# Two attentions per image on one core: own blocks mirrored from one half, and the last chunks of the second attention alternating with the next image's first chunks

## The chip, the cores and the metric

The kernel runs on one core of a Trainium2 chip. A core has a matrix engine (TensorE, PE in the profile; PEld is its loading of weights), VectorE (DVE), ScalarE (ACT), GpSimd (POOL) and SyncE (SP), which here only issues transfers. Transfers between the on-chip memory and DRAM (DMAs) are issued by an engine's instruction queue, here SP's almost always, and run on 16 DMA engines of the core. The metric is the device time of one execution, in microseconds (us). The median of three runs before the change is 1761.54 us (1758.81 to 1763.01).

## The reference

```python
B, C, S = 8, 128, 48;  N = S * S                     # 2304 positions
# layer 0: group norm, 32 rows of position table appended, q, k, v = leaky_relu(W x + b)
attn = einsum('bkn,bkm->bnm', q, k) / sqrt(128)      # masked to m <= n
out1 = einsum('bnm,bvm->bvn', softmax(attn) * mask, v);  x = x + out1
# layer 1, on tokens t of 128 channels
xh = layer_norm(t)
t = t + softmax(xh @ xh.T) @ xh                      # no mask: the matrix of logits is symmetric
wx = batch_norm(layer_norm(t) @ W.T)
y[i] = sigmoid(wx[i] + y[i-1] @ V.T)                 # recurrence over the 2304 tokens
t = t + y
```

Everything is fp32. Per image there are two attentions over 2304 positions, the first causal, the second full with a symmetric matrix of logits.

## The kernel before, in words

The 2304 positions are 18 blocks of 128, taken in six chunks (`NQ`) of three blocks (`QB`), 384 columns (`QC`). An attention's chunk j is a list of items. For each item TensorE makes the logits of one block of rows against the chunk's columns (tile `s`), ScalarE exponentiates them into one of six tiles `p`, and TensorE multiplies `p` with the values into the chunk's result `o` (one of two buffers). `Causal` does this for the first attention (L1018, L1020, L1029): its own three blocks are 384, 256 and 128 columns wide, GpSimd applies the triangle, and VectorE adds up the `p` for the sums of the softmax (L1040, L1044). `Full` does the second (L1217, L1219, L1231). There a block above the diagonal is computed once: VectorE transposes its exponentials in 32x32 pieces into a tile `t` (L1188), SP stores three such blocks to DRAM (`e`, L1168) and loads them back later in the order that completes the transpose (`g`, three buffers, L1159), and they serve as items "turned" of the later chunk, which need no logits (L1227). The three own blocks of a chunk, those on and beside the diagonal, are all computed directly at 384 columns: both halves.

The order of all instructions is written by the program itself. The items of all batches stand in one list, `stream`: causal chunks of a batch, then its full chunks, with the first three items of the next batch's first causal chunk set among the last six of the full part. The logits of an item are issued three items (`LAG`) ahead of its product. All other work (group norm, projection to q, k, v, normalization, transposed stores and loads, results) is in chains of steps; `Stream` keeps a model of the time and of when each engine is free, and runs a step when the model's time has come to it, or at once when an item needs it (`st.finish`). Each engine executes its own list in this order. A step that issues a DMA puts it at its place in the issuing engine's queue, where it waits for what it needs with all that stands behind it.

`project` makes q, k and v of a chunk (L879, L882, then an addition at L884 into a tile z and the leaky ReLU at L889), the first three of the next batch from full chunk 4 on. `Causal.after` takes a chunk's result: VectorE turns it (L958), SP stores and reloads it (`o_d`, `to_c`, L966 and L972) except for the last chunk, the residual and the layer norm follow (L1091, L920, L934), and TensorE transposes it into `xh` (L939, L1110). `xhT` and `xh` have one buffer, so the next batch's may be written only when the full part of this batch is done. `Full.after` copies the result (L1248), divides, adds the residual, and SP stores the turned tokens and reloads them (`t_d`, `rs`, then `t2x`, `scale`; L1291 to L1300) for the product with W (`wx`, L1306). After the eighth batch comes the recurrence.

Of the kernel before, what the change touches and what calls it, by code (L numbers as in the profile page):

```python
# [604 lines left out]
def fast_path(ctx: ExitStack, tc: tile.TileContext, x, pe, w_ffn, out, x_tok, w_qkv, w_pos, v_t, gamma_beta, flag):  # L605
# [61 lines left out]
    with ExitStack() as actx:  # L667
# [187 lines left out]
        def project(b, n):  # L855
# [18 lines left out]
            def part(j):  # L874
                def f():
# [7 lines left out]
                    z = chunk_tile("z", f"z_{b}_{n}_{j}")  # L883
                    nc.vector.tensor_add(z, ps[:, :QC], c["pb"][:, j, :])  # L884
# [3 lines left out]

                    nc.vector.scalar_tensor_tensor(dst, z, 0.01, z, ALU.mult, ALU.max)  # L889
# [97 lines left out]
        t1_tok, x_hat, normed_chunks = {}, {}, {}  # L987

        class Causal:
# [57 lines left out]
            def after(self, j, o):  # L1047
# [52 lines left out]
                def normed():  # L1100
                    if j == 0:
                        x_hat[b] = (
                            big.tile([P, NB, P], F32, tag="xhT", name=f"xhT_{b}"), big.tile([P, N], F32, tag="xh", name=f"xh_{b}")
                        )
# [7 lines left out]
                def shifted():  # L1112
# [4 lines left out]
                c["chain"] = normed_chunks[b, j] = st.add([  # L1117
# [6 lines left out]
                    (normed, 0.0, [("DVE", 1.1)]),  # L1124
                    (back, 0.35, [("ACT", 0.5)]),
                    (shifted, 0.0, [("POOL", 1.2)]),
                ], max(at, st.free["DVE"]) + 0.2 - st.now)

        class Full:
# [13 lines left out]
            def items():  # L1143
                chunks = []
                for j in range(NQ):
                    behind = list(range(j + 1, NQ))
                    ahead = [("direct", QB * n + g) for n in ([0] + behind if j == 0 else behind + [j]) for g in range(QB)]
# [3 lines left out]
                    chunks.append([w for _, w in sorted(both, key=lambda e: e[0])])  # L1151
                return listed(chunks)

            def load(self):
# [3 lines left out]
                for r in range(R):  # L1158
                    nc.sync.dma_start(  # L1159
                        g[ts(r, SQ)].rearrange("c a j m r -> c a (j m r)"),  # L1160
                        d.rearrange("(a c) b f -> b c a f", a=R)[r],
                    )
                self.loaded[i, j] = g

            def store(self):
                j, n, t, at = self.to_store.popleft()
                d = dpool.tile([P, R, QB * QB * SQ], F32, tag=f"e_{j}_{n}", name=f"e_{self.b}_{j}_{n}")
                nc.sync.dma_start(d, t.rearrange("p b j m r -> p b (j m r)"))  # L1168
                self.stored[j, n] = d, max(at, st.now)

            def prefetch(self):
# [3 lines left out]
                if n < len(self.pairs) and n < self.used + 3 and self.pairs[n] in self.stored:  # L1175
                    if self.stored[self.pairs[n]][1] + 6.0 <= st.now:
                        self.load()

# [17 lines left out]
            def begin(self, j, what, first):  # L1196
# [3 lines left out]
                if first and b + 1 < B:  # L1200
                    if j == 1:
                        norm_chain[b + 1] = st.add(group_norm(b + 1))
                    if j == NQ - 2:
# [3 lines left out]
                if what[0] == "turned":  # L1207
# [5 lines left out]
                    return self.loaded[i, j][:, :, g, :, :].rearrange("p a m r -> p m a r"), 0.0  # L1213
                m = what[1]
                xh = x_hat[b][1]
                s = psum_s(f"s1_{b}_{j}_{m}")
                nc.tensor.matmul(s[:, :QC], xh[:, ts(m, P)], xh[:, ts(j, QC)], start=True, stop=True)  # L1217
                p = pp.tile([P, QC], F32, tag="p", name=f"p1_{b}_{j}_{m}")
                nc.scalar.activation(p, s[:, :QC], AF.Exp, bias=shift)  # L1219
# [397 lines left out]
```

## Time and profile before

| what | us |
|---|---|
| median of the runs | 1761.54 |
| profiled execution, its own time | 1763.07 |
| its span, first to last instruction | 1761.4 |
| TensorE busy | 1733.7 (98%) |
| VectorE busy | 1159.5 (66%) |
| ScalarE busy | 718.9 (41%) |
| GpSimd busy | 321.0 (18%) |
| s of the second attention (L1217), 1008 passes | 409.3 |
| its o, direct (L1231), 1008 passes | 402.4 |
| its o, turned (L1227), 720 passes | 281.4 |
| VectorE's transposes for the turned blocks (L1188), 360 | 186.1 |

An fp32 matmul is two passes, and both are counted. Busy time of an engine is the union of its instructions; the end of a matmul is modelled, so that neighbours overlap in it, and the distance between starts tells more. The chain that ended last names at each step what released the work, so its shares say where time taken away is time gained. A wait that the profile puts down to an engine costs only where that engine is on the chain. The granted TensorE clock was 0.991 of full speed.

### The profile page before, as it was taken

To read this page: it belongs to the slowest core of one execution; us is meant where nothing else is said; L and a number is where in the kernel's file an instruction comes from. 1 tells how busy PE (TensorE), PEld (TensorE's weight loads), DVE (VectorE), ACT (ScalarE), POOL (GpSimd) and SP (SyncE) were. 2 spreads that over 40 slices of the span, in tenths; PEclk is the share of its full clock that TensorE was granted. 3 is DMA by queue.
4 is the path that set the end of the run, shared out by engine and by line. 5 is a ranking of instruction groups with operands and counts; after the bars stand their busy time and mean duration, and the time that the engine had idled before them with its cause. 6 is when DMAs were issued, how large, how long until landed. Compare 5 with 4: busy or idle time off the path is not lost.

```text
span 1761.4 us, 21442 instructions
## 1 busy us (share of the span) xinstructions
PE 1733.7 (98%) x6134; PEld 1082.0 (61%) x6135; DVE 1159.5 (66%) x3163; ACT 718.9 (41%) x1332; POOL 321.0 (18%) x397
## 2 busy tenths in 40 slices
PE   8999999999999999999999999999999999999986
PEld 5666666656666566666666566665666666665565
DVE  4875569655886459755696557864587556974357
ACT  2344334443344424443244433444344432444345
POOL 1131002300132001410024001320014100240006
PEclk7999999999999999999999999999999999999998
DMA  3415673157533684156731575335941568216768
GB/s 128 144 32 185 174 202 117 63 178 208 161 93 110 182 223 138 41 178 178 205 117 61 181 203 158 99 111 175 229 140 41 172 178 211 62 56 181 204 214 217
DMA packets 206050, 261.94 MB, mean 149 GB/s; under 512 B 90113, under 2 KB 175010, under 8 KB 205412
## 3 DMA queue, kind: packets, MB, share of 16 engines
q1 hardware_dynamic: 204972, 257.47, 50.3%
q0 software_dynamic: 720, 2.62, 1.0%
q8 instruction: 51, 0.84, 0.2%
q14 instruction: 75, 0.61, 0.1%
q10 hardware_dynamic: 232, 0.40, 0.1%
HBM read 150.24 MB, written 110.17 MB: 148 GB/s over the span
## 4 chain that ended last, share of the span: by engine, by line
PE 96%; DMA 1%; DVE 1%; SPq 1%; issue 0%; ACT 0%; POOL 0%; DVEq 0%; ACTq 0%; POOLq 0%
PE s L1217 18%; PE o L1231 18%; PE s L1018 17%; PE o L1029 17%; PE o L1227 13%; PE pj L879 4%; PE pj L882 2%; PE z L1530 2%; PE wx L1306 2%; PE tb L939 1%; PE of_t L939 1%; PE pb L837 0%; DMA x<-in_x_dram 0%; PE dn L1077 0%; DMA t2x<-t_d 0%; DMA out_dram<-r 0%
## 5 line engine op out<-in xcount | busy, mean ns | idle before, releaser
L1219 ACT ACTIVATE p<-s,shift 128x384 f32<-128x384 f32 x504 | 292.5, 580 | 519.0 <-PE s L1217 497.8
L1217 PE MATMUL s<-xh 128*128 128x384 f32 x1008 | 409.3, 488 | 0.0
L1020 ACT ACTIVATE p<-s 128x384 f32<-128x384 f32 (+2 forms) x504 | 231.0, 460 | 427.3 <-PE s L1018 349.3
L1231 PE MATMUL o<-p,xhT 128*128 128x384 f32 x1008 | 402.4, 486 | 1.1 <-ACT p L1219 1.1
L1018 PE MATMUL s<-q,k 128*128 128x384 f32 (+2 forms) x1008 | 382.9, 462 | 0.2 <-DVE k L889 0.2
L1029 PE MATMUL o<-p,vT 128*128 128x384 f32 (+2 forms) x1008 | 378.3, 457 | 0.0
L1227 PE MATMUL o<-g,xhT 128*128 128x384 f32 x720 | 281.4, 486 | 1.1 <-DMA g<-e 1.1
L1188 DVE STREAM_TRANSPOSE t<-p 128x384 f32<-128x384 f32 x360 | 186.1, 550 | 136.2 <-ACT p L1219 97.6
L1231 PEld LDWEIGHTS o<-p,xhT 128*128 128x128 f32 x1008 | 190.2, 190 | 129.2 <-ACT p L1219 1.7
L1217 PEld LDWEIGHTS s<-xh 128*128 128x128 f32 x1008 | 187.4, 190 | 119.5
L1029 PEld LDWEIGHTS o<-p,vT 128*128 128x128 f32 x1008 | 188.5, 191 | 116.1 <-POOL p L1023 3.0
L1018 PEld LDWEIGHTS s<-q,k 128*128 128x128 f32 x1008 | 182.3, 191 | 96.7 <-issue 1.3
L1044 DVE TENSOR_TENSOR acc<-acc,p 128x384 f32<-128x384 f32 (+2 forms) x408 | 213.4, 523 | 26.5 <-POOL p L1023 2.9
L1227 PEld LDWEIGHTS o<-g,xhT 128*128 128x128 f32 x720 | 134.1, 190 | 87.7 <-issue 1.8
L1023 POOL TENSOR_TENSOR p<-p,triu 128x128 f32<-128x128 f32 x144 | 77.8, 544 | 528.9 <-ACT p L1020 527.6
L884 DVE TENSOR_TENSOR z<-pj,pb 128x384 f32<-128x384 f32 x144 | 79.4, 551 | 137.5 <-PE pj L879 120.3
L1280 POOL TENSOR_TENSOR roots<-ve_f,mhalf 128x3 f32<-128x3 f32 x48 | 42.0, 876 | 500.7 <-DVE ve_f L923 500.7
L1114 POOL TENSOR_SCALAR xhT<-xhT 128x384 f32<-128x384 f32 x48 | 60.8, 1267 | 187.5 <-PE tb L939 187.5
L879 PE MATMUL pj<-xn,wT 128*128 128x384 f32 x192 | 80.6, 505 | 1.4 <-DVE xn L872 1.4
L1307 DVE TENSOR_TENSOR scale<-wx,scale 128x384 f32<-128x384 f32 x46 | 25.6, 556 | 69.2 <-PE wx L1306 59.9
L1258 DVE TENSOR_REDUCE dn<-of_t 128x3 f32<-128x384 f32 x48 | 26.6, 554 | 67.5 <-PE of_t L939 67.5
L1115 POOL TENSOR_SCALAR t1t<-t1t 128x384 f32<-128x384 f32 x48 | 61.3, 1277 | 0.0
(237 smaller groups left out, 1469.9 us busy)
## 6 DMA issues: line engine op xcount, KB each, us to landing
e<-t SPq DMA_DIRECT2D x120, 576.0 KB
g<-e SPq DMA_DIRECT2D x480, 144.0 KB
pb<-posb_d SPq DMA_DIRECT2D x46, 576.0 KB
t1t<-in_x_tok_dram SPq DMA_DIRECT2D x48, 192.0 KB
t_d<-tt SPq DMA_DIRECT2D x184, 48.0 KB
t2x<-t_d SPq DMA_DIRECT2D x46, 192.0 KB
scale<-rs SPq DMA_DIRECT2D x46, 192.0 KB
x<-in_x_dram SPq DMA_DIRECT2D x14, 576.0 KB
```

What stands on the lines that cost most here:

```text
L879: nc.tensor.matmul(ps[:, :QC], wT[:, j, :], xn, start=True, stop=True)
L884: nc.vector.tensor_add(z, ps[:, :QC], c["pb"][:, j, :])
L1018: nc.tensor.matmul(s[:, off:QC], keys[b][:, ts(m, P)], queries[b, j][:, off:], start=True, stop=True)
L1020: nc.scalar.activation(p[:, off:], s[:, off:QC], AF.Exp, scale=SCALE)
L1023: nc.gpsimd.tensor_mul(p[:, off : off + P], p[:, off : off + P], triu)
L1029: nc.tensor.matmul(o[:, off:QC], vals[b][:, ts(m, P)], p[:, off:], start=first, stop=last)
L1044: nc.vector.tensor_add(a[:, off:], a[:, off:], p[:, off:])
L1188: nc.vector.transpose(t[:, :, :, g, :].rearrange("p b j r -> p j b r"), p.rearrange("p (j b r) -> p j b r", j=QB, b=R))
L1217: nc.tensor.matmul(s[:, :QC], xh[:, ts(m, P)], xh[:, ts(j, QC)], start=True, stop=True)
L1219: nc.scalar.activation(p, s[:, :QC], AF.Exp, bias=shift)
L1227: nc.tensor.matmul(out_ap, xhT[:, QB * i + g, :], p, start=first, stop=last)
L1231: nc.tensor.matmul(o[:, :QC], xhT[:, what[1], :], p, start=first, stop=last)
```

## The change

Own blocks of a full chunk: the logits and products of the second and third own block are now made only at and above the diagonal, 256 and 128 columns wide as in the causal part (`Full.offset`). What lies below is the mirror image: VectorE transposes the parts of the first two own blocks in 32x32 pieces into a tile `tm` (`mirror`), ScalarE's queue issues a store to DRAM and four loads into a tile `gm`, as steps of a chain with 3.5 us of model time for each way, and two items "mirrored" at the chunk's end multiply them, 128 and 256 columns wide. The first own block is moved to the chunk's front.

Order: the last three full chunks (`AMONG`) alternate with the first three causal chunks of the next batch: full 3 with causal 0 set among its last six items, full 4, causal 1, full 5, causal 2. Therefore the next batch's projection starts at full chunk 2, and the normalization, transpose and shift of causal chunks 0 and 1 are held back until full chunk 5 is done (`held`, `release`).

The projection's addition writes to q, k or v itself and the leaky ReLU works in place; the tiles z give their room to `tm` and `gm`. For the turned blocks the reordering moves from the load to the store: four DMAs store `e`, one loads `g`.

```diff
-                    z = chunk_tile("z", f"z_{b}_{n}_{j}")
-                    nc.vector.tensor_add(z, ps[:, :QC], c["pb"][:, j, :])
...
+                    nc.vector.tensor_add(dst, ps[:, :QC], c["pb"][:, j, :])
+                    nc.vector.scalar_tensor_tensor(dst, dst, 0.01, dst, ALU.mult, ALU.max)
...
+        AMONG, held = 3, []
+        def release():
+            for b, j, chain, tokens in held:
+                st.finish(chain)
+                normed_chunks[b, j] = st.add(tokens, 0.3)
+            held.clear()
...
+                tokens = [(normed, 0.0, [("DVE", 1.1)]), (back, 0.35, [("ACT", 0.5)]), (shifted, 0.0, [("POOL", 1.2)])]
+                if b and j < AMONG - 1:
+                    c["chain"] = st.add(steps, wait)
+                    held.append((b, j, c["chain"], tokens))
+                else:
+                    c["chain"] = normed_chunks[b, j] = st.add(steps + tokens, wait)
...
+                    order_of = [w for _, w in sorted(both, key=lambda e: e[0])]
+                    first = order_of.index(ahead[0])
+                    order_of.insert(0, order_of.pop(first))
+                    chunks.append(order_of + [("mirrored", g) for g in range(1, QB)])
+            def offset(j, m):
+                return max(0, m - QB * j) * P if m < QB * (j + 1) else 0
...
-                for r in range(R):
-                    nc.sync.dma_start(
-                        g[ts(r, SQ)].rearrange("c a j m r -> c a (j m r)"),
-                        d.rearrange("(a c) b f -> b c a f", a=R)[r],
-                    )
+                nc.sync.dma_start(g.rearrange("p a j m r -> p (a j m r)"), d.rearrange("p a f -> p (a f)"))
...
-                nc.sync.dma_start(d, t.rearrange("p b j m r -> p b (j m r)"))
+                turned = d.rearrange("(b c) a f -> a c b f", b=R)
+                for r in range(R):
+                    nc.sync.dma_start(turned[r], t[ts(r, SQ)].rearrange("c b j m r -> c b (j m r)"))
...
+            def mirror(self, j, g, p, ready):
+                b, left = self.b, QB - 1 - g
+                if g == 0:
+                    self.tm = chunk_tile("tm", f"tm_{b}_{j}", bufs=1).rearrange("p (b q r) -> p b q r", b=R, q=QB)
+                first = g * (QB - 1)
+                nc.vector.transpose(
+                    self.tm[:, :, first : first + left, :].rearrange("p b q r -> p q b r"),
+                    p[:, (g + 1) * P :].rearrange("p (q b r) -> p q b r", q=left, b=R),
+                )
+                at = st.then(ready, [("DVE", 0.17 + left * 0.13)])
+                if g < QB - 2:
+                    return
+                gm = chunk_tile("gm", f"gm_{b}_{j}", bufs=1).rearrange("p (a q r) -> p a q r", a=R, q=QB)
+                d = dpool.tile([P, R, QB * SQ], F32, tag=f"m_{j % 2}", name=f"m_{b}_{j}")
+                def out_of():
+                    nc.scalar.dma_start(d, tm.rearrange("p b q r -> p b (q r)"))
+                def back_in(r):
+                    nc.scalar.dma_start(
+                        gm[ts(r, SQ)].rearrange("c a q r -> c a (q r)"), d.rearrange("(a c) b f -> b c a f", a=R)[r]
+                    )
+                steps = [(partial(back_in, r), 0.0, [("ACT", 0.4)]) for r in range(R - 1)]
+                steps = [(out_of, 0.0, [("ACT", 0.4), ("", 3.5)]), *steps, (partial(back_in, R - 1), 0.0, [("ACT", 0.4), ("", 3.5)])]
+                self.moved = st.add(steps, at + 0.6 - st.now)
...
-                    if j == NQ - 2:
+                    if j == 2:
                         st.finish(norm_chain[b + 1])
                         project(b + 1, 0)
...
+                if what[0] == "mirrored":
+                    st.finish(self.moved)
+                    return self.gm.rearrange("p a q r -> p q a r"), 0.0
...
+                elif what[0] == "mirrored":
+                    g = what[1]
+                    cols = g * P
+                    out_ap = o[:, :cols].rearrange("p (m a r) -> p m a r", m=g, a=R)
+                    nc.tensor.matmul(out_ap, xhT[:, QB * j + g, :], p[:, g - 1 : 2 * g - 1], start=first, stop=last)
...
+                if j == NQ - 1:
+                    release()
...
+            for j, chunk in enumerate(chunks_of(Full(b))):
+                stream += chunk
+                if j < NQ - AMONG or not among:
+                    continue
+                ahead = among.pop(0)
+                if j == NQ - AMONG:
+                    for k in range(QB):
+                        stream.insert(len(stream) - 2 * QB + k + 1, ahead[k])
+                    ahead = ahead[QB:]
+                stream += ahead
+            for chunk in among:
+                stream += chunk
```

## The prediction

> **What bounds the kernel now.** I read the shares of busy time first, then the chain that ended last:
>
> ```profile
> PE 1733.7 (98%) x6134; PEld 1082.0 (61%) x6135; DVE 1159.5 (66%) x3163; ACT 718.9 (41%) x1332; POOL 321.0 (18%) x397
> ...
> PE 96%; DMA 1%; DVE 1%; SPq 1%; issue 0%; ACT 0%; POOL 0%; DVEq 0%; ACTq 0%; POOLq 0%
> ```
>
> TensorE carries the chain. The table of stages (PE, PEld, DVE, ACT, POOL busy, then clock, DMA share, GB/s) says where it isn't full:
>
> ```profile
> 0.00:40.00 40.00, 34.83 (x112) 22.57 (x113) 17.47 (x41) 9.57 (x19) 7.18 (x32) 0.74 0.41 140
> 40.00:1700.00 1660.00, 1652.41 (x5805) 1020.52 (x5807) 1094.71 (x3046) 670.32 (x1211) 287.03 (x342) 1.00 0.51 145
> 1700.00:1761.40 61.40, 46.43 (x220) 38.89 (x218) 47.29 (x76) 39.06 (x102) 26.80 (x24) 0.90 0.80 246
> ```
>
> Between 40 and 1700 us 7.6 us are idle, so every column taken from TensorE is time gained and every new wait is time lost. Busy time overlaps, so I price matmuls by the distance between starts, here in the timeline (start, length, line):
>
> ```profile
> 106.18 0.59 PE L1018 MATMUL s<-q,k 128*128 128x256 f32 x2
> 106.61 0.81 PE L1029 MATMUL o<-p,vT 128*128 128x384 f32 x2
> ...
> 110.72 0.81 PE L1018 MATMUL s<-q,k 128*128 128x384 f32 x2
> 111.36 0.38 PE L1029 MATMUL o<-p,vT 128*128 128x128 f32 x2
> 111.58 0.81 PE L1018 MATMUL s<-q,k 128*128 128x384 f32 x2
> ```
>
> A matmul of two passes takes 0.43 us at 256 columns, 0.64 at 384, 0.22 at 128. Over the trace the median distance of a pass is 323, 216 and 111 ns. Last, the waits (total, times, longest):
>
> ```profile
> SPq L1168 <- DVE t L1188: 367.0, 70, 24.8
> SPq L1159 <- PE o L1227: 120.5, 64, 5.6
> SPq L972 <- DMA o_d_c<-ot_c: 32.3, 18, 4.9
> ACT p L1020 <- DVE acc L1040: 30.0, 14, 3.6
> PE o L1227 <- DMA g<-e: 1.1, 2, 0.9
> ```
>
> The stage of chunks 3 to 5 is also where memory is fullest (same columns as the stages above):
>
> ```profile
> 220.00:230.00 10.00, 10.00 (x37) 6.16 (x36) 5.39 (x12) 3.90 (x5) 0.60 (x1) 1.00 1.04 247
> ```
>
> SyncE's queue waits much, and it harms nobody: TensorE waited 1.1 us in all for reloaded blocks. ScalarE's exponentials waited up to 3.6 us for VectorE's sums (six p buffers, one of which each needs), and TensorE's three items of lead covered it.
>
> **What the Trainium skill says.** "Perfetto Trace Analysis", Identifying the Most-Contended Engine: matmul busy share misjudges pipelined matmuls; agreed, 486 ns busy against 323 ns apart. "TensorE: Matmul & The Clock Gate", Back-to-back issue gap: the gap grows with columns and has a small constant. The trace agrees in form at twice the slope (128 more columns cost about 106 ns). "DMA: Bandwidth & Descriptors", Anatomy of one DMA: waits sit on the issuing sequencer before dispatch; the 367 us above are that. The same page, Issuing engines are not separate DMA queues: DMAs of SP and ACT share the 16 engines; no run yet shows it, ScalarE having issued three DMAs at the start.
>
> **Part by part.** *Narrower own blocks.* A chunk's own three blocks were three s and three o matmuls of 384: 12 passes x 0.3235 = 3.88 us. Now s is 384, 256, 128, o the same, and two mirrored o matmuls have 128 and 256: 2 x (0.323 + 0.216 + 0.111) x 2 + 2 x (0.111 + 0.216) = 3.26. Saved 0.626 us x 48 chunks = 30.0 us. By the mean distances of 128 columns (130 and 122 ns) it is about 26; I take 30.
>
> *VectorE's transposes of 256 and 128 columns*: about 0.40 + 0.25 us (scaled from L1188's 0.55 for 384), 31 us in all on an engine 66% busy. Exponentials shrink (580 to 384 and 277 ns): 24 us less on ScalarE. *z left out*: the same two operations in place, nothing. *Store and load swapped* (store 4 DMAs, load 1, before 1 and 4): five issues of 0.43 us on SP as before. *Projection of the next batch's first chunks at chunk 2 instead of 4, two normalizations held back until chunk 5's last product*: the same instructions elsewhere. Their cover is VectorE's slack; x, which the projection needs, is loaded a whole causal part earlier (issue at 280.6 in the timeline, chunk 2 after 370), so that wait costs nothing. What the held work delays is in walk B.
>
> *Five DMAs per chunk on ScalarE's queue*: 5 x 0.43 = 2.2 us, hidden under the 519 us that it waits at L1219. But each waits too. In the changed program's order the DMAs of SP and ACT take eight semaphores in turn, and each issue waits until the one eight before has landed. Until now only SP's own were in that ring. Now SP waits for DMAs that stand in ScalarE's queue behind exponentials, and so behind TensorE; what is queued behind are SP's loads of g. That is what I expect to cost. The order has no times; I walk it with durations from the trace. Landings after issue (from the trace's semaphore events): o_d_c<-ot_c, the twin of the new store, median 2.0; to_c<-o_d_c, the twin of the new loads, 2.0 (three quarters under 3.1); pb<-posb_d, the twin of the new single g load (576 KB, 4608 bytes per partition), 3.63 at least, 4.43 median, 5.94 three quarters; t2x<-t_d 2.35 at least, 3.7 median.
>
> *Walk A, chunks 3 and 4* (zero: s of block 11 of chunk 3; causal chunk 0 stands in its tail). TensorE's matmuls up to s15 are 11 of 0.645 us, one of 0.43, two of 0.22: 8.0. Seven of 0.645 and one of 0.43 more to the causal chunk's second s: 12.9; three of 0.645 to s17: 14.9; two and a 0.22 to its third s: 16.4. ScalarE's new store stands behind the exponential of s15: issued 8.6, landed 10.7. Its four loads stand behind the others' exponentials: issued 13.4, 15.5, 16.7, 17.2, landed 15.4, 17.6, 18.8, 19.3. SP in turn: the t2l store waits for the first landing (10.7), the second rs for 15.4, the second t_d for 17.6, the fourth for 18.8, and of the four stores of e that follow at 0.44 each the last for 19.3. So load g_1_4 goes at 20.95, though its buffer is free from 10.6, and lands at 25.4. TensorE needs it at 24.9, but is late already: chunk 4's first o needs one of two o buffers, and the causal chunk's result leaves it through VectorE, which has the projection before that (last part projected at 17.7, then 4.3 us of VectorE's rows: 21.95, against 20.9). That is 1.0 lost, and g_1_4 is in time at 25.9. The last of the eight DMAs behind g_1_4 waits for its landing; g_2_4 goes at 26.2, lands at 30.6, and is needed at 28.7: 1.9. Sum 2.9 us (1.4 if loads take 3.63 each, 5.9 if 5.94).
>
> *Walk B, chunk 5 into causal chunk 2* (zero: end of causal chunk 1). Up to s17 there are 11 matmuls of 0.645, two of 0.43, one of 0.22: 8.2. So the new store goes at 8.6 and lands at 10.7; four loads 10.9 to 12.2, the last lands at 14.2. TensorE comes to the mirrored matmul after eight more of 0.645 and one of 0.22, at 13.55: 0.65 lost. The t_d stores queue on the same landings, t2x goes at 13.2 and lands near 16.5; the wx matmul would start at 15.0: together 1.5 (0.4 to 2.5). VectorE then waits for to_c (17.5) and has some 15.6 us to do (residuals 2.5 and 3.9, projection 4.5, two held normalizations 2.0, scale 1.1, sums and the rest) before the sum that frees the p buffer of causal chunk 3's first exponential: 33.1, and 0.6 for the exponential, where TensorE would be at 31.6: 2.1 more. Half of that may be won back by work placed elsewhere; I take 2.6 in all (0.4 to 5).
>
> Sum: seven batches x (2.9 + 2.6) = 38.5, the last batch's chunk 5 1.5: 40. Against the profiled execution: 1763.07 - 30 + 40 = 1773; the median of the runs is 1.5 lower: **1771**.
>
> **Rivals.** *Faster: the loads land in time.* If the queue of SP is ahead of my walk by 5 us, or loads land in 3 us, walk A costs nothing; if VectorE follows, B costs under 1.5. Then 1761.5 - 30 + at most 15: 1732 to 1747, point 1739. For it: the 1.1 us of g waits before, and the spread of chunks 3 to 5 over more time (1.04 above would fall). Against: SP is now tied to ScalarE. It decides below 4.3 us of stall per batch. *The gain is eaten: same.* Stalls near 4.3 us per batch, or short matmuls at 0.33 instead of 0.22 us as some are: about 1761. *Slower by DMA crowding*: held-back DMAs then come in a burst, some 2 MB in 5 us against the 247 GB/s of the stage above; g_2_4 lands another 3 us late, 1790.
>
> **How the numbers follow.** Main case (1764 to 1784) 0.48, crowding (above 1784) 0.14, same 0.10, faster 0.28. 0.2% (3.5 us) is about what a measurement tells from no change. Faster 0.28, same 0.10, slower 0.62. The range, 1738 to 1794, leaves about one in ten at each end.
>
> **What would show it.** Passes of L1217's successor at 384, 256 and 128 columns with 323, 216, 111 ns between starts (gain right). In chunk 4 of each batch the turned o matmul waits for DMA g: tens of us where 1.1 stood, and SPq waits for gm or m (walk A). The mirrored o matmul waits for DMA gm, wx for t2x, and exponentials of causal chunk 3 wait for acc beyond 4 us (walk B). If TensorE's idle time from 40 us to the last batch stays under 15 us, both walks are wrong and it is faster.

## The result, and the profile after

| | us |
|---|---|
| before, median (range) | 1760.17 (1758.35 to 1763.01) |
| after, median (range) | 1838.81 (1838.33 to 1840.51) |
| ratio, 95% interval | 1.0448 (1.0432 to 1.0464) |
| forecast | 1771 (1738 to 1794) |
| profiled execution after, span | 1836.6 |

The change makes the kernel 4.5% slower (the kernel before has one run more here than ahead of the prediction). That it would be slower was forecast, by how much was not: 79 us lost instead of 11, and the range was left by 45 us.

First the page of the changed kernel, shares of busy time and the chain that ended last:

```profile
PE 1735.2 (94%) x6327; PEld 1103.0 (60%) x6327; DVE 1187.4 (65%) x3259; ACT 697.2 (38%) x1332; POOL 316.2 (17%) x397
...
PE 75%; DMA 10%; DVE 10%; issue 2%; SPq 1%; ACT 1%; POOL 1%; ACTq 0%; DVEq 0%; POOLq 0%
```

TensorE's share of the chain fell from 96% to 75%; transfers and VectorE, 1% each before, hold 10% each. The table of stages (us, PE, PEld, DVE, ACT, POOL busy, clock, DMA share, GB/s), from 40 us to the last batch's end:

```profile
40.00:1770.00 1730.00, 1648.79 (x5959) 1036.95 (x5958) 1118.77 (x3136) 645.57 (x1207) 281.21 (x340) 0.99 0.51 149
```

TensorE is idle for 81.2 us where it was idle for 7.6. A second measure counts slow matmuls too: for every pass the distance to the next start beyond 323, 216 or 111 ns for its columns (where it is over 60 ns), summed over the trace. I call it TensorE's excess. It is 40.3 us before and 145.1 after. So 105 us of stalls came and 30 us of columns went: 75, which is the difference of the spans (1836.6 - 1761.4 = 75.2). The waits (total, times, longest) say for what:

```profile
PEld o L1275 <- DMA g<-e: 42.2, 19, 5.0
...
PE o L1275 <- DMA g<-e: 33.3, 12, 4.4
...
PE o L1283 <- DMA t2x<-t_d: 13.3, 4, 3.8
...
PE o L1283 <- DMA gm<-m: 6.9, 3, 3.2
```

The turned products, which waited 1.1 us for `g` before, wait 33.3 (weight loads wait with them, so the two aren't added), and the first mirrored product of chunk 5 waits for `gm` (where the profile names t2x, this was landing in the same half microsecond; the product itself reads `gm`, and in the third batch it starts at 697.50, when `gm` has landed, at 697.25, and t2x has not, 697.75). The excess by line: 43.7 us at the turned products (1.7 before), 26.9 at the mirrored ones, 15.1 at the products of causal chunks, 12.4 at the direct ones.

One occurrence shows it all. This is the chain of the changed kernel between chunks 4 and 5 of the third batch (start, length, what):

```profile
648.48 0.67 PE o L1283 x4
649.15 0.17 SPq L1174
649.43 5.12 DMA t2x<-t_d
654.61 6.10 DMA g<-e
660.76 0.91 PE o L1275 x2
661.67 0.90 PE wx L1367 x2
662.57 1.28 PE s L1265 x2
663.85 1.28 PE o L1287 x2
```

SP puts g_2_4 out at 654.61, in the moment in which t2x, issued eight transfers earlier, has landed (654.55). In the trace the transfers of SP and those of ScalarE carry the same eight completion semaphores in turn, those of GpSimd carry others. g_2_4 stood so far back because SP had been held before: by the trace's semaphore events its second `rs` store went at 643.73 and its fourth `t_d` store at 646.62, when quarters of `gm` had landed at 643.71 and 646.61, and all that followed then came in one burst. Over the whole run SP's queue was held 110 times, 162.7 us in all, by landings of `m` and `gm`, transfers of another queue; the longest groups:

```profile
SPq L1182 <- DMA gm<-m: 57.2, 49, 6.1
...
SPq L1398 <- DMA m<-tm: 48.1, 7, 7.3
```

The load of g_2_4 needs 6.10 us; TensorE has nothing to do meanwhile. And when it goes on, a matmul of 384 columns takes 1.28 us where it takes 0.65. The table of stages has the cause beside it:

```profile
649.00:655.00 6.00, 5.24 (x21) 3.31 (x21) 3.64 (x15) 1.32 (x3) 0.00 (x0) 1.00 0.77 221
655.00:661.00 6.00, 2.44 (x10) 1.30 (x9) 2.12 (x6) 1.60 (x2) 0.85 (x1) 1.00 1.04 402
661.00:667.00 6.00, 6.00 (x14) 3.30 (x14) 2.27 (x5) 1.61 (x2) 0.00 (x0) 0.72 0.64 229
```

The transfers move 402 GB/s while TensorE stands (the held-back ones come together, as one of the rivals had it; the DMA engines are as busy, 1.04, as in the fullest stretch shown of before, which moved 247 GB/s), and afterwards the granted clock is 0.72 in the mean of six microseconds: 0.50 from 661.9 to 665.3. The Trainium skill ("TensorE: Matmul & The Clock Gate", Part 1: The HAM clock gate) states that an idle window of about 3.4 us halves the clock until a busy window of that length has passed, and that the windows run freely. The trace agrees: 1.28 us is twice the usual length, the clock record has eleven stretches at half clock between 60 and 1750 us, nine of 3.41 us and two of 6.83, and of two waits of nearly the same length at the same place in two batches (3.09 us before 697.50, 3.07 before 1347.42) one was followed by a clock of 1.00, the other by 0.57:

```profile
697.50:701.00 3.50, 3.50 (x14) 2.42 (x15) 1.59 (x7) 1.90 (x3) 0.00 (x0) 1.00 0.23 52
1347.50:1351.00 3.50, 3.50 (x10) 2.52 (x11) 0.51 (x3) 1.70 (x3) 0.00 (x0) 0.57 0.29 74
```

Sixteen waits of TensorE between 60 and 1750 us are 2.9 us or longer, and eleven of them were followed by half clock, the shortest of 2.92 us, less than the skill's window; five were not, the longest of 3.69 us. In the changed kernel 62 passes between 60 and 1750 us have double length and cost 17.1 us above the usual; before there were 11, 1.5 us, and no stretch at half clock between 60 and 1749 us.

### The profile page after: what moved, and what is told of

The parts are those of the page before. It is cut to its first block, busy times and chain, and to the rows that moved or that the text cites. A ratio compares the mean times of both kernels' runs of the same rounds, so it can differ in the third digit from the quotient of the medians.

```text
span 1836.6 us, 22164 instructions
## 1 busy us (share of the span) xinstructions
PE 1735.2 (94%) x6327; PEld 1103.0 (60%) x6327; DVE 1187.4 (65%) x3259; ACT 697.2 (38%) x1332; POOL 316.2 (17%) x397
## 4 chain that ended last, share of the span: by engine, by line
PE 75%; DMA 10%; DVE 10%; issue 2%; SPq 1%; ACT 1%; POOL 1%; ACTq 0%; DVEq 0%; POOLq 0%
PE s L1265 15%; PE o L1287 15%; PE s L1024 13%; PE o L1035 13%; PE o L1275 7%; PE pj L879 3%; DMA g<-e 3%; DMA t2x<-t_d 2%; PE o L1283 2%; PE z L1600 2%; DMA gm<-m 1%; PE wx L1367 1%; PE pj L882 1%; DMA m<-tm 1%; DVE acc L1050 1%
## 5 line engine op out<-in xcount | busy, mean ns | idle before, releaser
L1267 ACT ACTIVATE p<-s,shift 128x384 f32<-128x384 f32 (+2 forms) x504 | 275.0, 550 | 583.6 <-PE s L1265 503.5
L1035 PE MATMUL o<-p,vT 128*128 128x384 f32 (+2 forms) x1008 | 378.1, 458 | 10.4 <-POOL p L1029 6.2
L1265 PE MATMUL s<-xh 128*128 128x384 f32 (+2 forms) x1008 | 382.6, 462 | 0.0
L1287 PE MATMUL o<-p,xhT 128*128 128x384 f32 (+2 forms) x1008 | 375.6, 461 | 6.1 <-ACT of L1309 4.4
L1275 PE MATMUL o<-g,xhT 128*128 128x384 f32 x720 | 281.6, 495 | 33.9 <-DMA g<-e 33.3
L1029 POOL TENSOR_TENSOR p<-p,triu 128x128 f32<-128x128 f32 x144 | 73.0, 509 | 376.4 <-ACT p L1026 375.6
L1085 DVE TENSOR_TENSOR ownc<-dn,mine 128x12 f32<-128x12 f32 x48 | 8.0, 167 | 163.5 <-PE dn L1083 163.5
L927 POOL TENSOR_TENSOR rs_c<-ve_c,mhalf 128x3 f32<-128x3 f32 x48 | 47.8, 996 | 307.1 <-DVE ve_c L921 307.1
L886 DVE TENSOR_TENSOR q<-pj,pb 128x384 f32<-128x384 f32 x48 | 26.5, 552 | 72.7 <-PE pj L879 67.7
```

What stands on the lines that cost most here:

```text
L1029: nc.gpsimd.tensor_mul(p[:, off : off + P], p[:, off : off + P], triu)
L1035: nc.tensor.matmul(o[:, off:QC], vals[b][:, ts(m, P)], p[:, off:], start=first, stop=last)
L1265: nc.tensor.matmul(s[:, off:QC], xh[:, ts(m, P)], xh[:, j * QC + off : (j + 1) * QC], start=True, stop=True)
L1267: nc.scalar.activation(p[:, off:], s[:, off:QC], AF.Exp, bias=shift)
L1275: nc.tensor.matmul(out_ap, xhT[:, QB * i + g, :], p, start=first, stop=last)
L1287: nc.tensor.matmul(o[:, off:QC], xhT[:, what[1], :], p[:, off:], start=first, stop=last)
```

## The experiments

The theory to test: the mirror's five transfers stand in the ring of eight completion semaphores that SP's and ScalarE's transfers take in turn, so that SP's loads of `g` wait for landings of ScalarE's. Rivals: the alternation itself, whatever issues the transfers; the single large load of `g`; the lateness of `gm` alone. All are edits of the changed kernel. The kernel before ran beside each group and stood between 1759.7 and 1760.6. Several ratios are within 2% of 1; all intervals but that of e10 leave out 1, so that these small differences are clear of the spread of the runs.

| run | edit | median us | ratio to before, 95% | TensorE's excess us |
|---|---|---|---|---|
| e1 | no alternation | 1804.5 | 1.0251 (1.0234 to 1.0268) | 110.7 |
| e2 | no mirror | 1815.6 | 1.0331 (1.0300 to 1.0362) | 86.0 |
| e3 | no swap | 1910.3 | 1.0851 (1.0833 to 1.0869) | 219.1 |
| e4 | mirror issued by GpSimd | 1818.2 | 1.0345 (1.0322 to 1.0368) | 120.0 |
| e5 | mirror without DRAM | 1746.8 | 0.9920 (0.9903 to 0.9936) | 55.2 |
| e6 | e5, no alternation | 1728.8 | 0.9828 (0.9812 to 0.9844) | 34.3 |
| e7 | no alternation, mirror, swap | 1784.6 | 1.0137 (1.0110 to 1.0164) | 62.7 |
| e8 | mirror on TensorE, no alternation | 1755.1 | 0.9970 (0.9957 to 0.9982) | 44.9 |
| e9 | two waits filled | 1825.6 | 1.0371 (1.0354 to 1.0388) | 103.8 |
| e10 | e8, own blocks in front | 1760.9 | 0.9998 (0.9988 to 1.0008) | 50.5 |
| e11 | GpSimd, no alternation, own in front | 1765.5 | 1.0033 (1.0019 to 1.0046) | 70.6 |
| e12 | e11, issued by ScalarE | 1812.9 | 1.0307 (1.0278 to 1.0337) | 120.2 |
| e13 | e11, own spread as in the change | 1782.6 | 1.0115 (1.0090 to 1.0141) | 88.3 |
| e14 | e11, issued by SP | 1844.5 | 1.0478 (1.0455 to 1.0500) | 151.7 |
| e15 | e8, loads of g earlier | 1750.6 | 0.9944 (0.9925 to 0.9963) | 39.0 |

**e1, no alternation.**

```diff
-        AMONG, held = 3, []
+        AMONG, held = 1, []
...
-                    if j == 2:
+                    if j == NQ - 2:
                         st.finish(norm_chain[b + 1])
```

> The changed kernel with the order of the items as before (only causal chunk 0 of the next batch, in the tail of the last full chunk, nothing held back, projection from full chunk 4); the mirrored blocks and the swapped store and load stay. Shared ring (SP's loads wait for the landings of ScalarE's transfers, my theory): those transfers stand in the same ring, so at least half of the new stalls stay, 1790 to 1815 us. Alternation (the causal chunks between take away the time in which the loads were made ready): the stalls of chunk 4 go, the mirrored matmuls still wait for gm about 3 us a batch, 1735 to 1760.

Measured 1804.5, as the shared ring has it. Taking the alternation out gains 34 us, but `g` is waited for as before (33.3 us again, in 22 waits instead of 12); the chunks' nearness is not what makes it late.

**e2, no mirror.** All own blocks at 384 columns, no mirrored items.

```diff
-                    chunks.append(order_of + [("mirrored", g) for g in range(1, QB)])
+                    chunks.append(order_of)
...
-                return max(0, m - QB * j) * P if m < QB * (j + 1) else 0
+                return 0
...
-                    elif g < QB - 1:
-                        self.mirror(j, g, p, ready)
```

> The changed kernel with all three own blocks at 384 columns and no mirrored items, so no transfers by ScalarE; alternation and swap stay. Shared ring: SP is as free as before and the stalls of g go, the 30 us of narrower blocks go too: 1760 to 1775. Alternation: the waits for g (44 us of the 105) stay and only those for gm go: 1815 to 1845.

Measured 1815.6, inside the alternation's range, yet not for its reason: the excess at the products of `g` fell from 43.7 to 3.6 us, as the ring has it, and other waits took their place. The waits of e2:

```profile
PE tb L937 <- ACT xh L1116: 22.7, 7, 3.3
...
PE o L1287 <- ACT p L1267: 10.8, 7, 1.6
...
PE dn L1083 <- DVE parts L1077: 7.2, 7, 1.0
```

Seven each, one per batch: the normalizations held back are released at the end of chunk 5, and TensorE's transposes of the second one (`tb`) wait for ScalarE's copy of the first. Both expectations missed this. It is a price of the alternation; the changed kernel shows no such wait, as I read it because its TensorE has stalled already, which no run tests.

**e3, no swap.** One store of `e`, four loads of `g`, as before the change.

```diff
-                nc.sync.dma_start(g.rearrange("p a j m r -> p (a j m r)"), d.rearrange("p a f -> p (a f)"))
+                for r in range(R):
+                    nc.sync.dma_start(
+                        g[ts(r, SQ)].rearrange("c a j m r -> c a (j m r)"),
+                        d.rearrange("(a c) b f -> b c a f", a=R)[r],
+                    )
```

(and in `store` the four issues are one: `nc.sync.dma_start(d, t.rearrange(...))`.)

> The changed kernel with one store of e and four loads of g, as before the change. Late single load (a load of 576 KB landed 5.4 us after issue where the four landed in 3.9): each of some 13 waits for g is 1.5 us shorter and several no longer long enough to halve the clock, 1800 to 1815. Shared ring and alternation: three more issues stand ahead of each needed block, so within 10 us of the changed kernel, 1830 to 1850.

Measured 1910.3: both missed, the first (the late single load) in sign. The single load lands later after its issue (5.38 us in the median against 3.88 for the four before), but it takes one turn in the ring instead of four: at the loads of `g` SP's queue waits 182 us for landings of other transfers in e3, and 37 in the changed kernel. The excess at the turned products is 128.4 us instead of 43.7. The group of the turned products in e3:

```profile
L1277 PE MATMUL o<-g,xhT 128*128 128x384 f32 x720 | 300.1, 522 | 103.2 <-DMA g<-e 102.8
```

**e4, the mirror's transfers issued by GpSimd.** Its transfers have eight semaphores of their own.

```diff
-                    nc.scalar.dma_start(d, tm.rearrange("p b q r -> p b (q r)"))
+                    nc.gpsimd.dma_start(d, tm.rearrange("p b q r -> p b (q r)"))
...
-                    nc.scalar.dma_start(
+                    nc.gpsimd.dma_start(
                         gm[ts(r, SQ)].rearrange("c a q r -> c a (q r)"), d.rearrange("(a c) b f -> b c a f", a=R)[r]
```

> The changed kernel with the five transfers of each mirror issued by GpSimd, whose transfers have eight semaphores of their own; nothing else. Shared ring: SP waits for its own transfers only, g_2_4 is issued some 4 us earlier and its stall and the halved clock after it go; gm stays about as late: 1780 to 1800. Alternation: as the changed kernel, or slower by GpSimd's slower issue, 1830 to 1850.

The waits of e4:

```profile
PE o L1283 <- DMA gm<-m: 42.6, 16, 4.8
...
PE o L1275 <- DMA g<-e: 3.8, 4, 2.6
```

`g` is in time now (33.3 to 3.8 us), and SP's queue waits for no `m` or `gm` any more, which is the ring's mark. But `gm` is later: issued by GpSimd, its store and loads land after 3.7 and 3.0 us in the median, where ScalarE's took 2.1 and 2.0. So only 20.6 us of 38 at `g` are kept: 1818.2, between the two expected ranges. Half right.

**e5 and e6, the mirror without DRAM**, with and without alternation (e6 adds the edit of e1). The mirrored products read the tile that VectorE wrote, so the mirrored blocks have their numbers in other rows.

```diff
-                gm = chunk_tile("gm", f"gm_{b}_{j}", bufs=1).rearrange("p (a q r) -> p a q r", a=R, q=QB)
-                self.gm = gm
+                self.gm = self.tm
...
-                steps = [(partial(back_in, r), 0.0, [("ACT", 0.4)]) for r in range(R - 1)]
-                steps = [(out_of, ...), *steps, (partial(back_in, R - 1), ...)]
-                self.moved = st.add(steps, at + 0.6 - st.now)
...
-                    st.finish(self.moved)
```

> The changed kernel without the mirror's way through DRAM: the mirrored products read the tile that VectorE's transposes wrote. Left out is the exchange of quarters of 32 partitions (so the mirrored blocks hold their numbers in other rows); matmuls, transposes, alternation and swap stay. Shared ring: the waits for g (44 us) and gm (27 us) and the halved clock after them go, 1740 to 1755. Alternation has a price of its own, as the run without mirrored blocks suggests (46 us more excess on TensorE than before): 1770 to 1785.

> As e5 (the exchange of quarters left out), with the order of the items as before the change. This measures the narrower own blocks with the swap alone. If the sum's 30 us are right, and the swap and the order of the own blocks cost nothing: 1727 to 1735. If the swap has a price: 1740 or more.

These two settle the sum. e6 is 30.9 us faster than the kernel before beside it (1759.68): the narrower blocks give what was forecast, VectorE's transposes are hidden, and the swap and the new order of the own blocks, which e6 has too, cost nothing there. Its stage table, which answers to the second line of the one shown of before:

```profile
40.00:1660.00 1620.00, 1614.38 (x5961) 1030.12 (x5959) 1118.23 (x3137) 647.29 (x1206) 274.99 (x341) 1.00 0.51 148
```

5.6 us idle where 7.6 were. e5 against e6 is the alternation's own price, 18.0 us; two waits of e5, one a batch each, hold 12.5 of it:

```profile
PE tb L937 <- DVE xhT L932: 8.5, 7, 1.8
...
PE o L1282 <- ACT of L1304: 4.0, 7, 0.6
```

And the changed kernel against e5 is the price of the way through DRAM: 92.0 us with alternation (1838.8 - 1746.8), 75.7 without (1804.5 - 1728.8). 1746.8 lies in the range of the first expectation; the alternation's price is less than half of what e2 had suggested.

**e7, own blocks in front only**: the edits of e1, e2 and e3 together.

> The changed kernel with no alternation, no mirror and no swap; what stays is the projection in place and the own blocks at a chunk's front where they stood at its end. If both cost nothing: 1757 to 1764. If the later stores of the turned blocks make their loads late: 1770 or more.

1784.6, the second case: the order has a price, 25 us, when `g` comes in four loads. The change moved all three own blocks of a chunk from its end to the first places among its direct items, not only the first one to the front, so the blocks to be stored are made later and, as I read it, loaded later (17.5 us of waits for `g`). With the single load that price is not seen: the excess at the turned products is 22.0 us here and 3.6 in e2, which has the single load and the same wide blocks (and the alternation). e6 has none of it either.

**e8, e10, e15, the mirror on TensorE.** No memory at all: transposes into PSUM and a copy by ScalarE.

```diff
             def mirror(self, j, g, p, ready):
+                tp = psum_t(f"mir_{b}_{j}_{g}")
+                for k in range(left):
+                    nc.tensor.transpose(tp[:, ts(k, P)], p[:, ts(g + 1 + k, P)], ident)
+                st.spend(left * P * US / 2, ready)
+                nc.scalar.copy(self.gm[:, first : first + left * P], tp[:, : left * P])
```

(with the edit of e1; `first` is g * (QB - 1) * P, VectorE's transposes and the transfers go, and the mirrored product reads `gm` column by column.) e10 puts the three own blocks ahead of all turned ones, e15 changes one number in `prefetch`:

```diff
-                    if self.stored[self.pairs[n]][1] + 6.0 <= st.now:
+                    if self.stored[self.pairs[n]][1] + 3.0 <= st.now:
```

> The mirrored blocks made on TensorE: three transposes of 128 columns a chunk into PSUM (111 ns each by the trace, 144 of them, 16 us) and copies by ScalarE, no memory; no alternation; the swap stays. Shared ring as the cause: 30 us gained, 16 us spent, no new stall: 1744 to 1752. If the waits had to do with the mirrored items as such (copies late, transposes waiting for one of two PSUM buffers): 1760 or more.

> As e8 (mirror by transposes on TensorE, no alternation) with all three own blocks at the chunk's front instead of spread among the turned ones. e8 waited 12 us for g, the first turned items of chunk 4 being early; here they come two items later: 1741 to 1748. If the later stores of e cost more: 1755 or more.

> e8 (mirror by transposes on TensorE, no alternation) with the loads of g allowed 3 us instead of 6 us of model time after their stores. e8's 12 us of waits for g come from loads placed late in SP's list: 1741 to 1749. If the loads then stand in SP's queue until the stores have landed, with others behind them: 1755 to 1765.

e8 lies between its two cases, 1755.1: the sum 30 - 16 holds in the main. It is missed by 9.4 us, and at the turned products stand 12.3 us of excess, with loads of `g` late by a microsecond in chunk 4. e10, 1760.9, takes most of that away (3.5 left) and pays elsewhere, so that it ends in its second case, though not for the reason given there: 4.9 us of waits of `of_t` for the mirror's copies, which hold one of two PSUM buffers, and 4.0 for `xh`. e15 comes between its two cases, nearer to the first: 1750.6, 0.56% faster than before, the best of the versions that compute the whole result. Its waits for `g`, 8.6 us in e8:

```profile
PE o L1257 <- DMA g<-e: 5.2, 5, 2.7
```

**e9, two waits filled.**

```diff
             def product(self, j, what, o, p, ready, first, last):
                 xhT = x_hat[self.b][0]
+                if self.b < B - 1 and (j, *what) in ((4, "turned", 2, 0), (5, "mirrored", 1)):
+                    idle(psum_s(f"fill_{self.b}_{j}"), 9)
```

> The changed kernel with nine dummy matmuls (2.0 us) just before two products that waited 3 to 4.5 us in each of seven batches: the first block of g_2_4 in chunk 4, the first mirrored one in chunk 5. No data comes sooner. If the waits are paid a second time because TensorE's clock is halved after a long idle time (62 passes at double length, 17 us in the changed kernel), it is faster by 8 to 15 us though work was added: 1824 to 1831. If the halved clock has another cause: 1836 to 1842. If the dummies delay what would release the wait: 1845 or more.

13.2 us faster, as the halved clock has it: three stretches at half clock are left of eleven, and 28 double-length passes with 5.7 us of 62 with 17.1. The same place in the third batch, in the timeline of the changed kernel:

```profile
660.76 0.91 PE L1275 MATMUL o<-g,xhT 128*128 128x384 f32 x2 [3.56 <-DMA g<-e]
661.51 1.06 PE L1367 MATMUL wx<-t2x,w1T 128*128 128x384 f32 x2
662.36 1.49 PE L1265 MATMUL s<-xh 128*128 128x384 f32 x2
```

and in e9's:

```profile
652.07 2.17 PE L1446 MATMUL fill<-ident 128*128 128x128 f32 x18
656.67 0.91 PE L1277 MATMUL o<-g,xhT 128*128 128x384 f32 x2 [2.44 <-DMA g<-e]
657.42 0.81 PE L1369 MATMUL wx<-t2x,w1T 128*128 128x384 f32 x2
658.07 0.81 PE L1265 MATMUL s<-xh 128*128 128x384 f32 x2
```

The data comes no sooner (2.17 us of dummies and 2.44 of waiting, where 3.56 were waited), but the matmuls after it have full speed.

**e11 to e14, who issues.** All three own blocks ahead of everything else in a chunk (except e13), no alternation, and one word changed at the mirror's transfers: `nc.gpsimd`, `nc.scalar` or `nc.sync`.

```diff
-                    ahead = [("direct", QB * n + g) for n in range(j, NQ) for g in range(QB)]
+                    own = [("direct", QB * j + g) for g in range(QB)]
+                    ahead = [("direct", QB * n + g) for n in range(j + 1, NQ) for g in range(QB)]
...
-                    chunks.append(order_of + [("mirrored", g) for g in range(1, QB)])
+                    chunks.append(own + order_of + [("mirrored", g) for g in range(1, QB)])
```

> The mirror through DRAM as in the change, issued by GpSimd (semaphores of its own), no alternation, all own blocks at the chunk's front, so that 9 us or more lie between the last transpose and the first mirrored product. Shared ring and too short a time for the way as the only causes: no stalls left, 1728 to 1738. If the way through DRAM costs something else (more packets, GpSimd's triangles delayed): 1745 or more.

> As e11 with the five transfers issued by ScalarE as in the change: the ring is shared again, all else equal. Shared ring: gm is in time, but the loads of g stand behind its landings, 20 to 40 us of waits for g: 1755 to 1775. If only the lateness of gm mattered: as e11, 1728 to 1740.

> e1 (the change without alternation) with the mirror's transfers issued by GpSimd; the own blocks spread as in the change. Shared ring: of the 44 us that e1 lost against the kernel before, about what the issuer was worth with the own blocks in front (47 us) goes: 1757 to 1765, and what is left above 1729 is the way through DRAM itself (gm late at the chunk's end). If the order at the front made the ring's price: within 15 us of e1, 1790 to 1805.

> As e11 and e12 with the five transfers issued by SP itself. If any five more transfers in SP's ring cost what they cost from ScalarE: within 10 us of e12, 1803 to 1823. If it is ScalarE's queue, in which they stand behind exponentials while SP waits for their landings: they are issued in SP's own order when their data is there, 1765 to 1785.

e11 lies in its second case, e12 above both of its own. They differ by 47.4 us and, in the code, by nothing but the issuer. In both `gm` is nearly in time (5.7 and 3.8 us idle before it), so it is not its lateness. Their groups of turned products, e11 first:

```profile
L1274 PE MATMUL o<-g,xhT 128*128 128x384 f32 x720 | 280.7, 490 | 9.8 <-DMA g<-e 9.5
```

and e12:

```profile
L1274 PE MATMUL o<-g,xhT 128*128 128x384 f32 x720 | 289.5, 502 | 39.4 <-DMA g<-e 39.3
```

The loads themselves are no slower (5.59 and 5.87 us from issue to landing in the median); they are issued later. The waits of SP's queue in e12 name the mirror's transfers:

```profile
SPq L1181 <- DMA m<-tm: 67.7, 10, 8.9
...
SPq L1181 <- DMA gm<-m: 30.1, 36, 4.4
```

In e11 no wait of SP's queue ends with `m` or `gm`. This is the ring, shown at its place: 40 us more excess before the turned products and 12 more before the products that read `t2x`, another load of SP's (15.9 against 4.1). That ScalarE's time is taken by the issuing is no rival, for TensorE waits 5.9 us for its exponentials in both. The ring cost more than expected, and e11 itself is 37 us above e6: 14.6 us of excess at `g`, 10.4 at the direct products, 7.4 at `gm`; what of it GpSimd's issuing makes and what the order in front isn't separated. e13 falls between its two cases: against e1 the issuer is worth 21.9 us with the own blocks spread, and `gm` is late (24.0 us of waits).

e14 contradicts both its expectations. SP in place of ScalarE is 31.6 us worse; the waits went from `g` (0.7 us) to `gm`. The waits of SP's queue in e14:

```profile
SPq L1211 <- DVE tm L1198: 144.7, 17, 16.6
...
SPq L1214 <- DMA m<-tm: 62.4, 25, 5.6
```

The store of `tm` stands in SP's one queue, behind others' waits and with others behind it. So, as I read these runs, the mirror needs a queue other than SP's and a ring of its own; ScalarE gives the first, GpSimd both.

One thing is not clean in these pairs. GpSimd moves the same bytes in fewer packets: 9216 in its queue (9936 less the 720 of e12) where ScalarE's has 34560. But in the traces the mirror's packets take about the same time, 61 us from GpSimd and 65 us from ScalarE in the mean of the 16 engines. Since landings of `g` hardly differ either, I hold the ring for the cause of most of the 47 us; ScalarE's transfers with semaphores of their own were not tried, and so a part of it may be the packets'.

## Why the prediction was wrong

The gain was right; the step that failed is the sum of the stalls, 40 us forecast and 105 measured as excess. The ring, the places of the waits and the times of issue were right. The landings that set the waits' length were not, what a long wait does to the clock stood in the sum at nothing, and the last batch was put too low:

| | in the sum, us | in the trace, us |
|---|---|---|
| TensorE's wait for g_2_4, batches 1 to 7 | 13.3 (7 x 1.9) | 26.8 |
| wait for `gm` in chunk 5, batches 1 to 7 | 4.6 (7 x 0.65) | 20.2 (six batches) |
| passes at half clock | 0 | 15.6 more than before |
| the last batch | 1.5 | 8.8 (three waits) |

These four are some 52 of the 65 us that were missing.

**Right: the gain.** "Saved 0.626 us x 48 chunks = 30.0 us": e6 measures 30.9, and the median distances after are 323, 216 and 111 ns as used. VectorE's transposes, 33.8 us in e6 where 31 were forecast, were hidden.

**Right: where, and when transfers are issued.** Both walks named the waits that came. Set against the third batch, with walk A's zero at 627.8 (the third causal s is at 644.19 and was put at 16.4):

| | forecast | measured |
|---|---|---|
| A: g_2_4 issued | 26.2 | 26.8 |
| A: g_2_4 landed | 30.6 | 32.9 |
| A: TensorE's wait for it | 1.9 | 3.6 |
| B: store of tm issued, landed | 8.6, 10.7 | 8.4, 10.9 |
| B: last load of gm issued, landed | 12.2, 14.2 | 12.3, 16.5 |
| B: t2x issued, landed | 13.2, 16.5 | 13.3, 17.0 |
| B: TensorE's wait for gm | 0.65 | 3.1 |

(B's zero is 680.7, so that TensorE is free for the mirrored product at 13.55, as forecast.) The issues are right within 0.6 us in this batch: the ring was walked correctly.

**Wrong: the landings.** Walk A took 4.43 us for the load of `g`, the median of the twin `pb`, and walk B 2.0 us for a quarter of `gm`, the median of the twin `to_c`. In their places they took 6.10 and 4.2. Those medians are taken over a whole trace in which memory is half busy. g_2_4 comes in the burst at 402 GB/s; in eight batches it took 5.8 to 6.9 us. The rival "slower by DMA crowding" had this, some 2 MB in 5 us, as a case of its own (0.14 against 0.48) and 19 us dearer; the two were one case.

For `gm` it is something else. Over the run a quarter's median is 2.0 us as forecast, and around the wait memory moves 228 GB/s only (692 to 698 us). But SP's load of `pb`, 576 KB, goes out at 692.48, just ahead of the last two quarters, and they land with it (696.86, then 697.06 and 697.25); the first two, ahead of it, took 1.85 and 2.23. Of the 192 quarters 13 took longer than 3.1 us, 4.2 to 5.3 each: the last two of chunk 5 in the first six batches, 0.07 to 0.63 us behind `pb`, and one in the last batch, issued together with a load of `g`. No other quarter was issued within 0.7 us behind a load of that size. In chunk 5 of batches 7 and 8 no `pb` comes there, the same quarters took 1.9 to 2.0 us, and TensorE did not wait for them. Walk B did not have this load in it.

**Wrong: a stall was priced once.** The walks counted a wait as lost time and no more. The waits came to 3 to 4.4 us, eleven of sixteen were followed by half clock, and double-length passes cost 15.6 us more than before; filling two waits (e9) gave 13.2 us back. The walks' own waits, 1.0 to 2.1 us each, are shorter than any that half clock followed here (2.92); it is the wrong landings that make this one.

**Wrong: the cover of the moved work.** "Their cover is VectorE's slack", at a price of 1.0 us a batch for the `o` buffer. The alternation alone costs 18.0 us (e5 against e6): the `o` buffer 0.7 us of excess a batch, held not by VectorE but by ScalarE's copy (`of`), and the released normalizations, for which TensorE's transposes wait 1.2 us a batch, a wait that the walk left out. Exponentials behind late sums, priced at 2.1 a batch and halved, came in the changed kernel as a wait of 1.05 us in the third batch (at 715.07), as halved. A second one of 0.86 us at 720.73 is another: GpSimd's triangle stands behind the held chunk's shift (`t1t`) in GpSimd's list, which the walk did not price; 6.2 us in seven batches.

**Wrong: "five issues as before".** The swap is not neutral once the ring is full: undone, it costs 71.5 us more (e3), as each load then takes four turns. And the move of all own blocks to the front, which the sum did not price, costs 25 us where `g` comes in four loads (e7). The prediction saw neither; the two offset each other in the change, so that this error did not make it slower.

**Wrong: the last batch at 1.5 us.** It has no alternation, but the way through DRAM: waits of 3.7 and 2.0 us before turned products and 3.1 before a mirrored one within 17 us (1728.8 to 1745.6).

In one line, with runs: 1760.2 - 30.9 (narrower blocks) + 18.0 (alternation) + 92.0 (way through DRAM) = 1839.3, measured 1838.8. The terms are differences of neighbouring runs, so they add up by construction and prove nothing by it; without the way through DRAM the alternation costs 18.0 us, with it 34.3. The forecast had 40 for the last two. Of the 92, moving the issue to GpSimd takes 20.6 away, with longer landings of `gm` set against it; the rest holds the lateness of `gm` and the half clock, and was not divided by runs.

## What to carry to other kernels

Before a second engine's queue is given transfers, look at which completion semaphores they share with the first: a slot waits for the landing before it, and with it everything behind it in the other queue; fewer, larger transfers on the path that is needed then matter more than their own landing time. Price a new transfer by the landings in its place and not by the trace's median: ask what large load is issued just ahead of it, by whichever queue. To a TensorE wait that may reach 3 us add about 1.5 us for the half clock after it (an estimate: 17.1 us over eleven stretches). Where a layout change is small, look for a way that leaves memory out: three 111 ns transposes per chunk kept 10 of the 31 us (e15), where the way through DRAM lost all of them and 44 more (e1).

## What was new about the hardware

- Of TensorE waits of nearly one length one (3.07 us) was followed by half clock and one (3.09 us) was not; dummy matmuls of 2.0 us in a wait, which free no data, made the kernel 13.2 us faster.
- SP's and ScalarE's transfers took one set of eight completion semaphores, and SP's queue stood 162.7 us waiting for landings of ScalarE's; issued by GpSimd, with semaphores of its own, they held SP not once (e4, e11).
- The same five transfers are 34560 packets from ScalarE and 9216 from GpSimd over the run, and their stores landed after 2.3 and 3.4 us in the median (e12, e11).
- Four quarters of one tile, issued within 1.4 us, landed after 1.85, 2.23, 4.50 and 4.21 us, the later two with a 576 KB load that another queue had issued between them; all 13 of 192 quarters that took over 3.1 us were issued beside such a load. The Trainium skill ("DMA: Bandwidth & Descriptors", Issuing engines are not separate DMA queues) has the two engines' transfers interleave on the same 16 engines; the trace agrees with it.
